# One half of a convolution moved from matmul taps to passes on VectorE, and a row of scales turned one step later

## The chip, the cores and the metric

The kernel runs on one core of a Trainium2 chip. The metric is the time of one execution on the device in microseconds (us). Every comparison takes executions of both kernels on the same chip in the same rounds. The runs of the kernel before lay 0.2 to 0.4% apart within one call (3428.75 to 3435.80 us in the closest, 3426.04 to 3440.02 us in the widest); the record lists every run used here as fast.

Engine names are the profile's: PE is TensorE (matmul), DVE is VectorE, ACT is ScalarE, POOL is GpSimd, SP is SyncE, which issues the transfers here. "px", "pb", "ls_in" and the like are tiles of the program. Line numbers (L938) are lines of the kernel in question and shift by a few between kernels.

## The reference, cut to what matters

The kernel computes two layers on a 4 x 128 x 64 x 64 input. The change lies in the middle: a two-directional state-space block on 4 sequences of 4096 tokens with 128 channels. For each direction:

```python
def _mamba3(x, in_proj, conv_w, conv_b, A_log, dt_bias, D, norm_w, out_proj):
    zxbcdt = x @ in_proj                                # 128 -> 256 (z) + 256 (x) + 64 (B) + 64 (C) + 4 (dt)
    z, xbc, dt = jnp.split(zxbcdt, [D_INNER, D_INNER + CONV_DIM], axis=-1)
    xp = jnp.pad(xbc, ((0, 0), (K - 1, 0), (0, 0)))
    conv = sum((xp[:, i:i + l, :] * conv_w[:, i] for i in range(K))) + conv_b      # K = 4 taps
    xbc = jax.nn.silu(conv)
    xh, Bm, Cm = jnp.split(xbc, [D_INNER, D_INNER + D_STATE], axis=-1)
    ...                                                 # dt, decays, the scan over chunks, gate, norm
t = t + (mamba(ln(t), fwd) + reversed(mamba(reversed(ln(t)), bwd)))
```

The 256 channels of x are two halves of 128, in two directions: four "halves of x" to be projected and convolved. A depthwise convolution behind a projection can be made in two ways. PE can run one matmul per tap, with the tap multiplied into the weights, on shifted inputs (four matmuls, no other work). Or PE projects once, and DVE adds the shifted, scaled copies (one matmul, one eviction on ACT, three passes on DVE).

## The kernel before: the parts that matter

The block runs as 128 steps of 128 tokens (32 steps, i = 0 to 31, for each of 4 sequences). Four steps j = 0 to 3 are a group; while a group is scanned, the projections of the next one are made. All projections and several small tiles share three PSUM buffers in turn (`ring`). The orders of PE and ACT are the program's; the orders of DVE and POOL are chosen by a scheduler when the kernel is built, and then fixed.

```python
def row_scales(nc, k, ps, tag, pool, src, mr, mem, parts=None):
    yield from row_statistics(nc, k, ps, tag, pool, src, mr, parts)   # ls_in: four transposes, then bn_stats on DVE
    n = mr.shape[1]
    pt = ps.tile([n, P], F32, tag=tag, name="rs_t")                   # the turn of the scales
    nc.tensor.transpose(pt, mr[:, :, 1], k.ident)
    ...                                                               # copied, written to DRAM

def open_sequence(b):                     # a generator: one piece per step, from i = 4 of the sequence before
    ...
        yield from row_scales(nc, k, ring, "big", wk, src, mr, mem)   # i = 4..7 statistics, i = 8 turn
        scales(b, mem)                                                # 8 transfers tl <- scale
        for _ in range(3):
            yield
    if b not in ready:
        yield from scaled(b)                                          # 8 products tl x t on POOL
        yield
    yield from steps(b, ready[b])                                     # the "dt work": pd, pdt, pcs, pr

# forward halves: four tap matmuls each
def project_fwd(gr, c):
    px = ring.tile([P, MG], F32, tag="big", name="px")
    for tap in range(KC):
        nc.tensor.matmul(px, w[0]["x"][:, tap, bass.ts(c, P)], tl[:, rows(g, 0, tap)], ...)
    nc.scalar.activation(gr["x"][0][:, c, :], px, AF.Silu, bias=...)

# backward halves: one matmul, three passes
def project_bwd(gr, c):
    px = ring.tile([P, MG], F32, tag="big", name="px")
    nc.tensor.matmul(px, w[1]["x"][:, bass.ts(c, P)], tl[:, rows(g, 1, PAD)], start=True, stop=True)
    ...                                                               # memset, eviction, 3-column addition
    for n in range(1, KC):
        v = x[:, PAD - n : PAD - n + MG]
        nc.vector.scalar_tensor_tensor(v, px, taps[:, PAD - n : KC - n], v, ALU.mult, ALU.add)

# the deal over the steps of a group
if j == 0:   project_bwd(next, 0); project_bc(next, 0); project_fwd(next, 0)
elif j == 1: project_bwd(next, 1); means(...); project_bc(next, 1)
elif j == 2: project_fwd(next, 1); activate_bwd(next); project_z(...) x 4
```

In every step PE runs the state matmul, four transposes of x, the product y from lt and xdt, the product y from ct and S, and then "small" (L991), which must wait until DVE has updated the state S (L1029). Three sequences out of four are prepared during the one before (row statistics, turn, scaling, dt work: i = 4 to 21), and after a sequence has ended its output's row statistics are taken for the last layer (i = 20 to 28 of the next one, `ended`).

## Time and profile before

| | before |
|---|---|
| time, median of the rounds with the changed kernel | 3436.31 us (3430.04 to 3440.71, 4 runs) |
| span of the profiled run, granted clock | 3440.8 us, 0.980 |
| recurrent part | about 1934 to 3275 us |
| PE / DVE busy over the span | 95% / 62% |

The busy shares only say that PE is nearly always at work. What PE waits for is in the view of waits. Here it is for the recurrent part, 1935 to 3225 us of the kernel before (waiting line, what released it, us in total, times, longest):

```profile
PE small L991 <- DVE S L1029: 15.1, 29, 1.4
PE pdt L821 <- DVE xT L938: 8.1, 3, 2.7
PE ls_in L83 <- DVE xT L938: 7.0, 5, 2.0
...
PE pr L879 <- DVE ms L1089: 5.4, 3, 2.6
```

All the waits listed in this view total 55 us of 1290. What costs is which of them are long: pdt and pr are dt work, three times each (once for each coming sequence), and the clock falls behind them: after the wait of 2.71 us for pdt at 2123.76 us four transposes took 1.11 us, after one of 1.04 us at 2332.39 us they took 0.66 us (both in the profile lines of the prediction, below). "Half speed" and "half clock" stand below for such stretches, in which PE's instructions took 1.7 to 1.8 times as long as at other times (the y product from lt in the same step 1.98 us, otherwise 1.09); "full speed" stands for the other times.

A group's length is taken here from the start of its first px to the start of the next group's. Undisturbed groups of the last sequence take 39.7 to 40.3 us; those with row statistics 43 to 46; those in which dt work runs 49 to 51.

### The profile page before, as it was taken

Reading aid. Unit: us, or ns where it says so; the run is one execution under the profiler, and the core shown is the slowest. Engines: PE = TensorE matmul, PEld = TensorE weight load, DVE = VectorE, ACT = ScalarE, POOL = GpSimd, SP = SyncE. Lnnn points to the kernel's source line nnn. Section 1 sums busy time; section 2 is a strip of 40 time slices with the busy share of each in tenths; the row PEclk is TensorE's granted clock in tenths of the full one; section 3 lists DMA queues with packets and bytes.
Section 4 is the critical chain, followed back from the end, with each engine's and each line's share of the span. In section 5 each row is a group of like instructions: output and inputs, shape, how many; then the busy total and the mean of one; then the engine's idle time right before and its main releaser. Section 6 shows DMA issues by size and latency. Waiting matters only on the chain. (4 is left out here: it accounts for less than half of the span.)

```text
span 3440.8 us, 43618 instructions
## 1 busy us (share of the span) xinstructions
PE 3261.0 (95%) x16823; PEld 1717.0 (50%) x16823; DVE 2138.7 (62%) x3204; ACT 1557.9 (45%) x2060; POOL 1593.3 (46%) x1414
## 2 busy tenths in 40 slices
PE   7999999999999999999998899999999999999976
PEld 2554545555555555455554344444444444544445
DVE  7555445555545555455544676777677777777767
ACT  3323233323333333333322566666656566666556
POOL 3434332534343424242533265557446654565653
PEclk9999999999999999999999899999999999999988
DMA  4000000000000000000001233333333423333332
GB/s 164 1 1 1 1 1 1 0 1 1 1 1 1 0 1 1 1 1 1 1 1 48 74 111 80 96 87 111 86 81 96 111 80 81 95 94 89 85 109 99
DMA packets 91685, 162.71 MB, mean 47 GB/s; under 512 B 23822, under 2 KB 27534, under 8 KB 90316
## 3 DMA queue, kind: packets, MB, share of 16 engines
q1 hardware_dynamic: 90252, 158.53, 16.2%
q8 instruction: 134, 2.20, 0.3%
q10 hardware_dynamic: 1216, 1.31, 0.1%
q14 instruction: 83, 0.68, 0.1%
HBM read 149.97 MB, written 9.82 MB: 46 GB/s over the span
## 5 line engine op out<-in xcount | busy, mean ns | idle before, releaser
L369 ACT ACTIVATE ex<-pf 128x1024 f32<-128x1024 f32 x512 | 497.0, 1021 | 571.6 <-PE pf L367 559.3
L384 DVE TENSOR_TENSOR es<-es,ex 128x1024 f32<-128x1024 f32 x448 | 590.6, 1318 | 207.5 <-ACT ex L369 179.4
L367 PE MATMUL pf<-theta,phi 64*128 64x512 f32 x2048 | 513.3, 619 | 10.8 <-ACT ex L369 10.4
L319 PE MATMUL pm<-yf,w 128*128 128x256 f32 x2048 | 503.1, 380 | 0.0
L378 PE MATMUL acc<-ex,gT 128*64 128x512 f32 x2048 | 491.4, 606 | 0.2 <-ACT ex L369 0.2
L331 POOL TENSOR_TENSOR eo<-s 128x256 f32<-128x256 f32 x128 | 90.1, 725 | 782.4 <-ACT s L328 782.4
L319 PEld LDWEIGHTS pm<-yf,w 128*128 128x128 f32 x2048 | 383.9, 189 | 113.5 <-issue 54.3
L367 PEld LDWEIGHTS pf<-theta,phi 64*128 64x128 f32 x2048 | 174.0, 186 | 326.7 <-ACT ex L369 208.6
L1007 POOL TENSOR_TENSOR ct<-ct,Cst 128x512 f32<-128x512 f32 x128 | 181.3, 1417 | 323.0 <-DMA ct<-csmem 261.9
L334 DVE TENSOR_TENSOR eo<-eo,pm 128x512 f32<-128x512 f32 x64 | 44.0, 688 | 425.8 <-PE pm L319 397.1
L378 PEld LDWEIGHTS acc<-ex,gT 128*64 128x64 f32 x2048 | 127.5, 136 | 337.5 <-issue 327.2
L969 DVE TENSOR_TENSOR lt<-cs,lt 128x1024 f32<-128x1024 f32 x128 | 180.5, 1411 | 182.3 <-DMA lt<-csmem 171.7
L328 ACT COPY s<-pm 128x512 f32<-128x512 f32 x64 | 37.5, 585 | 498.6 <-PE pm L319 498.6
L286 POOL TENSOR_TENSOR yf<-yr 128x340 f32<-128x340 f32 x256 | 241.4, 963 | 4.9
L914 PE MATMUL px<-tl,wx_fwd 128*128 128x512 f32 x512 | 238.6, 609 | 0.0
L901 PE MATMUL pb<-tl,wbc_bwd 128*64 128x512 f32 x512 | 235.1, 601 | 0.0
L901 PE MATMUL pb<-tl,wbc_fwd 128*64 128x512 f32 x512 | 234.5, 601 | 0.0
L286 POOL TENSOR_TENSOR yr<-xp 128x700 f32<-128x700 f32 x64 | 100.4, 1569 | 277.8 <-PE pm L319 232.0
L1072 POOL TENSOR_TENSOR yT<-yT,zT 128x512 f32<-128x512 f32 x127 | 183.8, 1456 | 74.1 <-DVE yT L1059 58.7
L1006 DVE TENSOR_TENSOR lt<-lt,gm 128x1024 f32<-128x1024 f32 x128 | 187.6, 1465 | 1.3
L390 DVE RECIPROCAL att<-den 128x512 f32<-128x512 f32 x32 | 107.4, 3357 | 108.0 <-PE den L388 108.0
L319 PE MATMUL pm<-yr,w 128*128 128x256 f32 x512 | 162.6, 398 | 0.0
(263 smaller groups left out, 5488.1 us busy)
## 6 DMA issues: line engine op xcount, KB each, us to landing
lt<-csmem SPq DMA_DIRECT2D x128, 512.0 KB, 5.5
ct<-csmem SPq DMA_DIRECT2D x256, 128.0 KB, 5.3
rs<-m SPq DMA_DIRECT2D x31, 512.0 KB, 3.7
t<-in_x SPq DMA_DIRECT2D x4, 2048.0 KB, 28.5
rows<-after SPq DMA_DIRECT2D x32, 256.0 KB, 4.8
out<-t SPq DMA_DIRECT2D x4, 2048.0 KB, 11.4
tl<-scale SPq DMA_DIRECT2D x24, 256.0 KB, 6.4
w<-in_w7t SPq DMA_DIRECT2D x1, 3136.0 KB
```

The source lines that it names most:

```text
L286: nc.gpsimd.tensor_tensor(out, at(x), at(y), op)
L319: nc.tensor.matmul(pm[:, e, :], wt, src, start=(i == 0), stop=(i == len(terms) - 1))
L367: nc.tensor.matmul(pf[:, e, :], phi[HALF[e], m, :], th[HALF[e]], start=True, stop=True)
L369: nc.scalar.activation(ex, pf, AF.Exp, scale=scale)
L378: nc.tensor.matmul(acc[HALF[e]], gT[:, 2 * m + e, :], ex[:, e, :], start=(m == 0), stop=(m == NT // 2 - 1))
L384: nc.vector.tensor_tensor(es, es, ex, ALU.add)
L901: nc.tensor.matmul(out, w[i]["bc"][:, tap, bass.ts(c, DS)], src, start=(tap == 0), stop=(tap == KC - 1),)
L914: nc.tensor.matmul(px, w[0]["x"][:, tap, bass.ts(c, P)], tl[:, rows(g, 0, tap)], start=(tap == 0), stop=(tap == KC - 1),)
L969: nc.vector.tensor_tensor(m["lt"], m["b"]["cs"][:, :, m["i"], :].unsqueeze(3).to_broadcast([P, ND, NHEAD, P]), m["lt"], ALU.subtract,)
L1006: nc.vector.tensor_tensor(lt, lt, gm.unsqueeze(2).to_broadcast([P, ND, NHEAD, P]), ALU.mult)
L1007: nc.gpsimd.tensor_tensor(m["ct"], m["ct"], Cs[:, cols].unsqueeze(1).to_broadcast([P, NHEAD, P]), ALU.mult)
L1072: eng.tensor_tensor(v, v, gr["z"][d][:, :, half(d, j // 2)], ALU.mult)
```

## The change

The intent was to take 192 matmul instructions off PE, which is busy 95% of the span, give DVE the three passes instead, and to let the scales' turn come a step later, when its input is sure to be there. The diff, cut to its core:

```diff
 def row_scales(...):
     yield from row_statistics(nc, k, ps, tag, pool, src, mr, parts)
+    yield
     n = mr.shape[1]
...
-        def project_fwd(gr, c):
+        def project_fwd(gr):                      # forward half 0 alone keeps four taps
...
-        def project_bwd(gr, c):
+        def project(gr, i, c):                    # backward 0 and 1, forward 1
+            wx = w[1]["x"][:, bass.ts(c, P)] if i else w[0]["x1"]
+            nc.tensor.matmul(px, wx, tl[:, rows(g, i, PAD)], start=True, stop=True)
...
             for n in range(1, KC):
-                nc.vector.scalar_tensor_tensor(v, px, taps[:, PAD - n : KC - n], v, ALU.mult, ALU.add)
+                nc.vector.scalar_tensor_tensor(at(n), px, taps[:, PAD - n : KC - n], at(n), ALU.mult, ALU.add)
...
             if j == 0:
-                    project_bwd(groups[G + 1], 0)
+                    project(groups[G + 1], 1, 0)
+                    project(groups[G + 1], 0, 1)
                     project_bc(groups[G + 1], 0)
-                    project_fwd(groups[G + 1], 0)
...
             elif j == 2:
-                    project_fwd(groups[G + 1], 1)
-                    activate_bwd(groups[G + 1])
+                    project_fwd(groups[G + 1])
+                    for i, c in STEPS_X:          # (1, 0), (0, 1), (1, 1)
+                        activate(groups[G + 1], i, c)
```

The one added `yield` sits in a generator. Everything after it in the same generator moves one step later too: the eight transfers of the scales, the eight products on POOL, and the dt work. So the change has two parts: the convolution (C), and the delay (Y), which is itself three delays for each coming sequence. The same helper also turns the scales for the last layer (`ended`); those turns move one step as well, and so do the scales of the first sequence, before the loop.

More of the change, by code (lines that the diff above doesn't have):

```diff
@@ L762, in mamba @@
                 s["z"] = wp.tile([P, DI], F32, name="wz_" + d)
-                s["x"] = wp.tile([P, DI] if i else [P, KC, DI], F32, name="wx_" + d)
+                s["x"] = wp.tile([P, DI] if i else [P, KC, P], F32, name="wx_" + d)
                 s["bc"] = wp.tile([P, KC, 2 * DS], F32, name="wbc_" + d)
@@ L770, in mamba @@
                     if i == 0:
-                        nc.gpsimd.tensor_tensor(s["x"][:, c, :], f[:, DI : 2 * DI], cw[i][:, c, 0:DI], ALU.mult)
+                        nc.gpsimd.tensor_tensor(s["x"][:, c, :], f[:, DI : DI + P], cw[i][:, c, 0:P], ALU.mult)
                 if i:
                     nc.scalar.copy(s["x"], f[:, DI : 2 * DI])
+                else:
+                    s["x1"] = wp.tile([P, P], F32, name="wx1")
+                    nc.scalar.copy(s["x1"], f[:, DI + P : 2 * DI])
                 nc.scalar.copy(s["z"], f[:, 0:DI])
@@ L906, in project_bc @@
             act() if later is None else later.append(act)
-        def project_fwd(gr, c):
+        def project_fwd(gr):
             tl, g = gr["tl"], gr["at"][1]
-            if c == 0:
-                gr["x"][0] = grp.tile([P, 2, MG], F32, tag="x0", name="xT0")
             px = ring.tile([P, MG], F32, tag="big", name="px")
             for tap in range(KC):
-                nc.tensor.matmul(
-                    px, w[0]["x"][:, tap, bass.ts(c, P)], tl[:, rows(g, 0, tap)],
-                    start=(tap == 0), stop=(tap == KC - 1),
-                )
-            nc.scalar.activation(gr["x"][0][:, c, :], px, AF.Silu, bias=w[0]["cb"][:, c : c + 1])
@@ L920, in project_bwd @@
-        def project_bwd(gr, c):
+                nc.tensor.matmul(px, w[0]["x"][:, tap, :], tl[:, rows(g, 0, tap)], start=(tap == 0), stop=(tap == KC - 1))
+            nc.scalar.activation(gr["x"][0][:, 0, :], px, AF.Silu, bias=w[0]["cb"][:, 0:1])
+        def project(gr, i, c):
             tl, g = gr["tl"], gr["at"][1]
-            if c == 0:
-                gr["x+"] = grp.tile([P, 2, PAD + MG], F32, tag="x1", name="xT1")
-                gr["x"][1] = gr["x+"][:, :, PAD:]
             px = ring.tile([P, MG], F32, tag="big", name="px")
-            nc.tensor.matmul(px, w[1]["x"][:, bass.ts(c, P)], tl[:, rows(g, 1, PAD)], start=True, stop=True)
-            x = gr["x+"][:, c, :]
-            taps = w[1]["taps"][:, c, :]
-            nc.vector.memset(x[:, 0:PAD], 0.0)
-            nc.scalar.activation(x[:, PAD:], px, AF.Identity, scale=taps[:, PAD:KC], bias=w[1]["cb"][:, c : c + 1])
+            wx = w[1]["x"][:, bass.ts(c, P)] if i else w[0]["x1"]
+            nc.tensor.matmul(px, wx, tl[:, rows(g, i, PAD)], start=True, stop=True)
+            x = gr["x+"][i][:, c, :]
+            taps = w[i]["taps"][:, c, :]
+            at = lambda n: x[:, PAD - n : PAD - n + MG] if i else x[:, n : n + MG]
+            nc.vector.memset(x[:, 0:PAD] if i else x[:, MG:], 0.0)
+            nc.scalar.activation(at(0), px, AF.Identity, scale=taps[:, PAD:KC], bias=w[i]["cb"][:, c : c + 1])
@@ L933, in project_bwd @@
             if g:
-                v = x[:, MG : MG + PAD]
-                nc.vector.tensor_tensor(v, v, groups[gr["at"][0] * NG + g - 1]["x+"][:, c, 0:PAD], ALU.add)
+                v = x[:, MG:] if i else x[:, 0:PAD]
+                past = groups[gr["at"][0] * NG + g - 1]["x+"][i][:, c, :]
+                nc.vector.tensor_tensor(v, v, past[:, 0:PAD] if i else past[:, MG:], ALU.add)
             for n in range(1, KC):
-                v = x[:, PAD - n : PAD - n + MG]
-                nc.vector.scalar_tensor_tensor(v, px, taps[:, PAD - n : KC - n], v, ALU.mult, ALU.add)
@@ L940, in activate_bwd, with activate @@
-        def activate_bwd(gr):
-            for c in range(2):
-                x = gr["x"][1][:, c, :]
-                nc.scalar.activation(x, x, AF.Silu)
+                nc.vector.scalar_tensor_tensor(at(n), px, taps[:, PAD - n : KC - n], at(n), ALU.mult, ALU.add)
+        def activate(gr, i, c):
+            x = gr["x"][i][:, c, :]
+            nc.scalar.activation(x, x, AF.Silu)
         def project_z(gr, i, c):
@@ L1102, in means @@
             )
+        STEPS_X = ((1, 0), (0, 1), (1, 1))
         def outputs(gr, d):
@@ L1174, in open_group @@
         def open_group(G):
-            groups[G] = dict(at=(G // NG, G % NG), tl=ready[G // NG], x={}, bc={}, z={}, y=([], []))
+            x = [grp.tile([P, 2, PAD + MG], F32, tag=f"x{i}", name=f"xT{i}") for i in range(ND)]
+            groups[G] = {
+                "at": (G // NG, G % NG), "tl": ready[G // NG], "bc": {}, "z": {}, "y": ([], []), "x+": x,
+                "x": [x[0][:, :, 0:MG], x[1][:, :, PAD:]],
+            }
         def open_step(n):
@@ L1194, in mamba @@
             act()
-        for c in range(2):
-            project_bwd(groups[0], c)
-        for c in range(2):
-            project_fwd(groups[0], c)
-        activate_bwd(groups[0])
+        for i, c in STEPS_X:
+            project(groups[0], i, c)
+        project_fwd(groups[0])
+        for i, c in STEPS_X:
+            activate(groups[0], i, c)
         differences(m[0])
@@ L1235, in mamba @@
                 if more:
-                    project_bwd(groups[G + 1], 1)
+                    project(groups[G + 1], 1, 1)
                 if G > 0:
@@ L1242, in mamba @@
                 if more:
-                    project_fwd(groups[G + 1], 1)
-                    activate_bwd(groups[G + 1])
+                    project_fwd(groups[G + 1])
+                    for i, c in STEPS_X:
+                        activate(groups[G + 1], i, c)
                 for i in range(ND):
```

## The prediction

> **What bounds the kernel now.** I read the page first, then the busy time stretch by stretch, then the groups of instructions, and last the timelines of TensorE (PE) and VectorE (DVE) in one group of the part that the change touches, with the chain that ended last beside them.
>
> ```profile
> PE 3261.0 (95%) x16823; PEld 1717.0 (50%) x16823; DVE 2138.7 (62%) x3204; ACT 1557.9 (45%) x2060; POOL 1593.3 (46%) x1414
> 2000.00:2400.00 400.00, 383.52 (x2526) 196.16 (x2526) 296.73 (x544) 248.77 (x331) 239.69 (x186) 0.99 0.36 99
> ```
>
> The first line is the whole span. The second is one stretch of the recurrent part (about 1935 to 3300 us, the only part the change touches apart from the moved turn of the scales); its columns are length, then busy PE, PE weight load, DVE, ACT, POOL, then granted clock, DMA share and GB/s. There PE is busy 383.5 of 400 us and DVE already 296.7 (74%). So PE bounds the part, but DVE has only a quarter free, and the average hides single steps. The part is 32 groups of four steps. In each group the convolved x of the next group is made: the forward half by four tap matmuls each, the backward halves by one matmul and three passes on DVE.
>
> ```profile
> L914 PE MATMUL px<-tl,wx_fwd 128*128 128x512 f32 x509 | 237.3, 609 | 0.0
> L938 DVE SCALAR_TENSOR_TENSOR xT<-px,taps_bwd,xT 128x512 f32<-128x512 f32 x192 | 142.7, 745 | 7.2 <-ACT xT L932 4.2
> ```
>
> A logical tap matmul shows as two instructions (32 groups x 2 halves x 4 taps x 2 = 512). Next, the chain through a group's first step (start, us, what), and DVE in the same step:
>
> ```profile
> 2231.71 0.26 PE small L991
> 2231.97 0.42 PE small L993 x4
> 2232.39 1.06 PE px L928 x2
> 2233.45 3.60 PE pb L901 x16
> 2237.04 3.63 PE px L914 x8
> ...
> 2243.46 0.26 PE small L991
> ```
>
> ```profile
> 2231.81 2.06 DVE L969 TENSOR_TENSOR lt<-cs,lt 128x1024 f32<-128x1024 f32 x1
> 2236.76 1.63 DVE L969 TENSOR_TENSOR lt<-cs,lt 128x1024 f32<-128x1024 f32 x1
> 2238.31 0.74 DVE L938 SCALAR_TENSOR_TENSOR xT<-px,taps_bwd,xT 128x512 f32<-128x512 f32 x1
> 2241.37 0.42 DVE L1029 TENSOR_TENSOR S<-S,small 128x256 f32<-128x256 f32 x1 [2.32 <-PE small L1017]
> ```
>
> PE takes 11.75 us from one L991 to the next with no gap. The next L991 needs the state update S (L1029) on DVE; S waited 2.32 us for PE and ended at 2241.79, 1.67 us before PE wanted it. DVE's slack in this step is therefore 2.32 + 1.67 = 4.0 us. In the second and third step there is none: PE is tied to the transfer of lt (the chain has a DMA of 5.3 to 5.7 us there, followed by DVE work and then PE).
>
> [...]
>
> ```profile
> 2123.76 1.11 PE L821 MATMUL pdt<-ident,pds 128*128 128x128 f32 x4 [2.71 <-DVE xT L938]
> 2124.81 1.12 PE L1017 MATMUL small<-xdtd,bt 128*64 128x256 f32 x4
> ...
> 2332.39 0.66 PE L83 MATMUL ls_in<-ident,t 128*128 128x128 f32 x4 [1.04 <-DVE xT L938]
> 2332.98 0.65 PE L1017 MATMUL small<-xdtd,bt 128*64 128x256 f32 x4
> ...
> 3261.86 0.40 PE L101 MATMUL rs_t<-ident,mr 128*32 128x128 f32 x1 [5.38 <-POOL mr L74]
> ```
>
> After 1.04 us idle four transposes take 0.66 us; after 2.71 us they take 1.11 and everything is slow for some 5 us, which adds 2.5 to 3 us. [...] beside GpSimd's additions L969 took 2.06 and 1.63 us instead of 1.23, while the passes with px in PSUM (L938) stay at 730 to 755 ns throughout. [...] the passes here follow each other at 0.66 us (2238.31 to its end is 0.74, the next row could start earlier), so I use 0.66 us on the path.
>
> **The change part by part.** Forward half 1 loses three of four taps: 3 x 2 instructions at 0.43 us (eight L914 in 3.63 us less the fill, L901 pairs start every 0.43) = 2.58 us of PE per group, 82.6 us over 32. That is the ceiling, 2.4%. Against it, per group: DVE gains three passes (3 x 0.745), a three-column addition (0.16 alone) and a memset (0.06) = 2.5 us; ACT gains 0.78 (Identity eviction) + 0.62 (Silu in place) − 0.69 (Silu eviction) = 0.71 us. DVE then holds about 30 + 2.5 = 32.5 us of a group of some 37.4, so what counts is which step gets it.
>
> First step. PE work is now one px, one px, pb: 11.75 − 2.58 = about 9.1 us. By the built program's order, DVE runs between two S: xdt, xdtd, lt difference, gm, the lt product, a pass, a second lt difference, then four passes (two per projection, taken in turns), then S; the sixth pass follows S. The second difference cannot start before its transfer, 5.1 us after the first L991 (2236.76 − 2231.64), takes 1.6, then 4 x 0.66 and S 0.4: 9.8 us. So the step becomes DVE-bound at about 9.85 us: gain 1.9, not 2.58.
>
> Second step: the same PE work, with the sixth pass at its start, where DVE has waited 3.2 us for a transfer. All passes but one now come after S, and the next px (third step) takes the PSUM buffer that they read: it can start 0.1 us sooner to 0.3 later. About 0.
>
> Third step: px for forward half 0 and the four z. The fourth z waits for the eviction of the first, behind three instead of two in-place Silu: +0.57 us on ACT, of which about 0.4 reach PE. Loss 0.4. Fourth step unchanged.
>
> A group without row statistics: 1.9 − 0.4 = 1.5 to 1.6 us. There are 22 such among the 31 that project for a successor: 22 x 1.6 = +35 us.
>
> Nine groups also take row statistics (three with two sets a step, six with one). There PE transposes four blocks (ls_in) after the projections, in one of three PSUM buffers. Before, that buffer was released early in the first step, because 3.6 us of forward taps lay between. Now PE arrives 6.2 us after L991 and the buffer is the first projection's, read until its third pass, about 8.8 to 9.2 us. PE idles some 2.9 us, past the length that cost the clock above; then four transposes, state, turn and y run at half speed. First steps of 12.2 to 12.6 us become about 15. Nine times −2.7 = −24 us.
>
> Before the loop: weights on GpSimd halved (3.72 us for four, PE waited 1.89 for them) and six matmuls less at a cold clock, nine passes instead of six: about +3 us.
>
> The moved turn of the scales: only at 3261.86 did it cost anything, 5.38 us idle and about 3 us of slow clock; one step later the input is ready: +8 us. It also moves the dt work of a sequence one step later, off the step where it waited 2.7 us for passes, onto ones where it waits for others: 0.
>
> Sum: 35 − 24 + 3 + 8 = 22 us. 3434.6 − 22 = about 3412 us, −0.65%.
>
> **The rivals.** (a) All of PE's saving counts: 82.6 + 8 = 91 us, 3344 us. For it: PE is busy 96%, and the 4.0 us of DVE slack exceeds the 2.5 added. Against: PE's own shortening of 2.58 uses up that slack too (4.0 − 2.58 − 1.7 before S is below zero). (b) DVE becomes the bound everywhere: each group loses what the first step gains and statistics groups lose 3 to 4 us with the clock: 3450 to 3460. For it: 74% average, several DVE instructions stretched to 2.3 us by GpSimd. Against: in plain groups DVE still waits 2 to 3 us for transfers in three of four steps. (c) The clock stays up[...]: statistics groups lose 0.5 instead of 2.7, 3392.
>
> **Range and chances.** The sum rests on 35 ± 12 and −24 ± 14[...]. I take 3412, with 3382 to 3440 for 8 in 10. Faster by over 2% (below 3365.9) needs nearly all of the ceiling: 0.05. Slower by over 2% (above 3503) would need DVE to bind in every step and the clock to fall in most: 0.02. Within: 0.93.
>
> **What would show it right or wrong.** Right: PE matmul instructions fewer by 192; plain groups of about 38 us instead of 39.7; in their first step L991 waits for S (L1028 in the changed kernel) by up to 1 us; in statistics groups ls_in waits 2.5 to 3.5 us for a pass on px, and the four transposes after it take 1.1 us; no wait of 5 us before the last turn of the scales. Wrong: plain groups at 37.2 us (then DVE had more room than I counted), or over 39 us (then the third step's px waits for the passes), or statistics groups at the old 43 to 46 us.

## The result, and the profile after

| | before | after |
|---|---|---|
| median (range, runs) | 3436.31 us (3430.04 to 3440.71, 4) | 3410.97 us (3404.29 to 3415.20, 4) |
| profiled span, clock | 3440.8 us, 0.980 | 3412.4 us, 0.977 |

The ratio of after to before is 0.9926, 95% interval 0.9901 to 0.9951. Ratios here are the mean time of one kernel's fast runs over that of the other's in the same rounds, so not quite the ratio of the medians. The time, 25 us less, is almost exactly the predicted 3412; it falls in the class "within 2%", which was given 0.93. The terms of the sum are another matter.

The page of after, busy time of the span:

```profile
PE 3188.1 (93%) x16631; PEld 1685.0 (49%) x16631; DVE 2194.7 (64%) x3360; ACT 1573.9 (46%) x2090; POOL 1610.2 (47%) x1414
```

The stretch 2000 to 2400 us of after (length, PE, weight load, DVE, ACT, POOL, granted clock, DMA share, GB/s):

```profile
2000.00:2400.00 400.00, 365.50 (x2467) 187.69 (x2467) 312.45 (x589) 251.09 (x336) 245.73 (x189) 0.97 0.37 99
```

PE has exactly 192 instructions fewer (16823 to 16631). It is busy 18 us less in this stretch and DVE 16 us more, and the granted clock has gone from 0.99 to 0.97. PE now waits longer (98 us in all the waits listed for 1935 to 3225 us, 55 in before), and after some of its waits it runs at half speed, as the lines further down show.

The group of instructions that was moved, in after: DVE's passes by tile (busy, mean ns, idle before).

```profile
L938 DVE SCALAR_TENSOR_TENSOR xT<-px,taps_bwd,xT 128x512 f32<-128x512 f32 x192 | 141.7, 738 | 4.3 <-ACT xT L932 4.0
L938 DVE SCALAR_TENSOR_TENSOR xT<-px,taps_fwd,xT 128x512 f32<-128x512 f32 x96 | 70.8, 738 | 0.0
```

The 96 new passes take 70.8 us of DVE, each 738 ns, like the old ones. Four in a row start 0.66 us apart (3034.34, 3035.00, 3035.66 and 3036.32 us in the step below).

An undisturbed plain group's first step in after (steps 8 to 11 of the last sequence; start, duration, instruction, idle time before it), first PE, then DVE in the same step:

```profile
3028.05 1.13 PE L927 MATMUL px<-tl,wx_bwd 128*128 128x512 f32 x2
3029.02 1.02 PE L927 MATMUL px<-tl,wx 128*128 128x512 f32 x2
...
3033.45 0.61 PE L1016 MATMUL small<-xdtd,bt 128*64 128x256 f32 x4
...
3037.44 0.33 PE L990 MATMUL small<-ident,Bst 128*128 128x128 f32 x1 [1.17 <-DVE S L1028]
```

```profile
3034.34 0.74 DVE L938 SCALAR_TENSOR_TENSOR xT<-px,taps_bwd,xT 128x512 f32<-128x512 f32 x1
...
3036.32 0.74 DVE L938 SCALAR_TENSOR_TENSOR xT<-px,taps_fwd,xT 128x512 f32<-128x512 f32 x1
3036.97 0.41 DVE L1028 TENSOR_TENSOR S<-S,small 128x256 f32<-128x256 f32 x1
3037.30 0.74 DVE L938 SCALAR_TENSOR_TENSOR xT<-px,taps_fwd,xT 128x512 f32<-128x512 f32 x1
```

The state matmul that S needs ends at about 3034.06. S starts only at 3036.97, right behind four passes, and PE waits 1.17 us for it. The step shrank from 11.76 us to 10.07, and the group from 39.72 to 38.64.

The waits of PE in after, same window as before:

```profile
PE ls_in L83 <- DVE xT L938: 27.4, 11, 3.4
PE small L990 <- DVE S L1028: 23.8, 18, 2.8
PE y L1046 <- POOL ct L1006: 18.4, 3, 6.3
```

The first two were expected. The third was not: three waits of 6 us for a product on POOL, one in each sequence during which the next one is prepared. What stands ahead of that product on POOL, and the issue of the transfers on SP:

```profile
2034.73 7.23 SPq L110 DMA_DIRECT2D tl<-scale  x8
2042.36 1.09 SPq L961 DMA_DIRECT2D ct<-csmem  x2
```

```profile
2042.36 5.25 POOL L728 TENSOR_TENSOR tl<-tl,t 128x512 f32<-128x512 f32 x4 [8.97 <-DMA tl<-scale]
...
2052.13 2.12 POOL L728 TENSOR_TENSOR tl<-tl,t 128x512 f32<-128x512 f32 x2
...
2054.79 1.26 POOL L1006 TENSOR_TENSOR ct<-ct,Cst 128x512 f32<-128x512 f32 x1
```

All eight products of the delayed scaling run from 2042.36 to 2054.2, and the ct product that PE needs comes behind them, at 2054.79. PE gets it at 2056.1, after 6.31 us idle, and then runs at half speed for about 5 us (this y product took 1.13 us, otherwise 0.67; the two px matmuls at 2058.30 took 2.07 us, otherwise 1.13). The transfer of ct is not what it waited for: its second half was issued at 2042.99, and the page of after has a median of 5.3 us from issue to landing of ct, so it was there at about 2048.3 (an estimate from these two numbers). What stood in the way is POOL's order: an idle wait of 8.97 us for the transfers of the scales, and then the products.

Two more lines of after, for the row statistics in a first step and for the last turn (PE):

```profile
1975.06 1.09 PE L83 MATMUL ls_in<-ident,t 128*128 128x128 f32 x8 [3.14 <-DVE xT L938]
1976.08 1.12 PE L1016 MATMUL small<-xdtd,bt 128*64 128x256 f32 x4
...
3234.29 1.11 PE L83 MATMUL ls_in<-ident,t 128*128 128x128 f32 x4 [4.24 <-POOL t L1150]
...
3242.29 0.30 PE L102 MATMUL rs_t<-ident,mr 128*32 128x128 f32 x1
```

The wait of 3.14 us and the half clock behind it (1.12 us where 0.65 is full speed) are as predicted. The last turn (rs_t) no longer waits 5.38 us, but the row statistics of the last sequence in the step where it used to stand now wait 4.24 us for an addition on POOL, and PE runs at half speed behind it (1.11 us for the four transposes, otherwise 0.66).

The table that carried the rest of the study adds up group lengths of the profiled runs by place in the sequence, over the sequences listed (the last group listed is that of steps 20 to 23 of the last sequence). "Start" is the start of the first group; it moved by up to 5 us between runs with the same convolution code before it, so that much of a profile's span is scatter. Each column is one execution, and not always a typical one: the profiled execution took 6.3 us more than the median of its kernel in before (3442.57 us), 3.3 more in after, 10.4 more in "+ late turn", 4.1 less in "dt later", and lay within 2 us of it in the other four. A few us in one row are therefore no evidence by themselves.

| steps | before | after | Y alone | C alone | dt later | C + dt later | + late turn | S first, plain |
|---|---|---|---|---|---|---|---|---|
| 0-3 | 156.0 | 157.2 | 155.6 | 156.7 | 155.5 | 159.0 | 157.7 | 156.8 |
| 4-7 | 176.7 | 178.8 | 177.2 | 181.4 | 177.6 | 177.4 | 180.5 | 177.0 |
| 8-11 | 163.5 | 173.9 | 171.1 | 158.6 | 162.5 | 160.4 | 173.9 | 157.9 |
| 12-15 | 161.8 | 165.2 | 167.2 | 159.1 | 159.5 | 159.1 | 164.0 | 157.9 |
| 16-19 | 191.5 | 165.5 | 175.1 | 194.7 | 179.1 | 162.9 | 162.5 | 159.6 |
| 20-23 | 185.2 | 183.9 | 187.3 | 169.0 | 186.0 | 183.9 | 187.4 | 185.8 |
| 24-27 (3 sequences) | 126.7 | 123.6 | 126.8 | 124.4 | 126.9 | 124.4 | 122.7 | 121.8 |
| 28-31 (3 sequences) | 117.3 | 111.6 | 117.3 | 109.6 | 116.0 | 110.2 | 111.8 | 110.1 |
| sum | 1278.9 | 1259.6 | 1277.6 | 1253.4 | 1263.1 | 1237.3 | 1260.6 | 1226.8 |
| start | 1934.1 | 1927.8 | 1929.6 | 1929.8 | 1929.3 | 1930.7 | 1932.8 | 1930.1 |

Before to after, the largest entries are not where the convolution should act: 26 us gained in steps 16 to 19, 14 us lost in steps 8 to 15. That gave theory R: Y is two opposite effects, the dt work moved to better steps and the scaling moved ahead of a ct product. Its rival is P, the sum as predicted: Y worth 8 us at the last turn, nothing else.

### The profile page after: what moved, and what is told of

It is laid out like the page before. It is cut to its first block, busy times and chain, and to the rows that moved or that the text cites. A ratio compares the mean times of both kernels' runs of the same rounds, so it can differ in the third digit from the quotient of the medians.

```text
span 3412.4 us, 43419 instructions
## 1 busy us (share of the span) xinstructions
PE 3188.1 (93%) x16631; PEld 1685.0 (49%) x16631; DVE 2194.7 (64%) x3360; ACT 1573.9 (46%) x2090; POOL 1610.2 (47%) x1414
## 5 line engine op out<-in xcount | busy, mean ns | idle before, releaser
L368 PE MATMUL pf<-theta,phi 64*128 64x512 f32 x2048 | 511.9, 618 | 12.4 <-ACT ex L370 12.0
L1006 POOL TENSOR_TENSOR ct<-ct,Cst 128x512 f32<-128x512 f32 x128 | 207.5, 1621 | 318.2 <-DMA ct<-csmem 281.3
L329 ACT COPY s<-pm 128x512 f32<-128x512 f32 x64 | 37.5, 585 | 496.9 <-PE pm L320 496.9
L968 DVE TENSOR_TENSOR lt<-cs,lt 128x1024 f32<-128x1024 f32 x128 | 172.8, 1350 | 124.8 <-DMA lt<-csmem 124.6
L1071 POOL TENSOR_TENSOR yT<-yT,zT 128x512 f32<-128x512 f32 x127 | 175.2, 1388 | 60.5 <-DVE yT L1058 44.8
L1038 PE MATMUL y<-lt,xdt 128*64 128x128 f32 x2048 | 146.4, 287 | 6.6 <-DVE lt L1005 3.4
```

What stands on the lines that cost most here:

```text
L368: nc.tensor.matmul(pf[:, e, :], phi[HALF[e], m, :], th[HALF[e]], start=True, stop=True)
L968: nc.vector.tensor_tensor(m["lt"], m["b"]["cs"][:, :, m["i"], :].unsqueeze(3).to_broadcast([P, ND, NHEAD, P]), m["lt"], ALU.subtract,)
L1006: nc.gpsimd.tensor_tensor(m["ct"], m["ct"], Cs[:, cols].unsqueeze(1).to_broadcast([P, NHEAD, P]), ALU.mult)
L1038: nc.tensor.matmul(y[HALF[h], d, c, at[d]], m["dt"][:, d, 2 * c + h, :], m["lt"][:, d, 2 * c + h, :], start=(i % 2 == 0 and c == 0), stop= ...
L1071: eng.tensor_tensor(v, v, gr["z"][d][:, :, half(d, j // 2)], ALU.mult)
```

## The experiments

Twelve kernels ran in four calls, each call on one chip with its own runs of the kernel before. Later calls are compared with "C + dt later" through the ratios to before.

### 1. Y alone

```diff
 # kernel before
     yield from row_statistics(nc, k, ps, tag, pool, src, mr, parts)
+    yield
```

> The kernel before with nothing but the one-step delay of the scales (no work of x moved). Theory P, the sum in the prediction: the delay is worth about 8 us (a wait of 5.4 us at the last turn and about 3 us of slow clock behind it), and neither the dt work nor the multiplication by the scales matters, so about 3428 us, ratio 0.9977. Theory R, read from the trace of after: the delay moves three things of one chain, and gains about 25 us in the groups of steps 16 to 19 (dt work), loses about 16 us in the groups of steps 8 to 15 (C waits about 6 us for GpSimd behind the scaling), and gains about 8 us at the end: about 3417 to 3421 us, ratio 0.995 to 0.9965. R also expects two or three waits of some 6 us of the y product for the C product on GpSimd; P expects none.

Measured: 3435.18 us against 3434.09 of before; ratio 1.0009 (0.9996 to 1.0023). The delay is worth nothing, so both theories were too hopeful. The column shows why it is zero: 16.4 us gained in steps 16 to 19, 13.0 lost in steps 8 to 15, 2.1 lost in steps 20 to 23. The loss that R named is there, but not by the wait that it named: there is no wait for ct in this run's view of waits. Another instruction stands behind the delayed scaling here, the first half of S's update (L1027). POOL, then DVE, in steps 8 to 11 of the first sequence of this kernel:

```profile
2049.85 3.18 POOL L728 TENSOR_TENSOR tl<-tl,t 128x512 f32<-128x512 f32 x3
2052.99 0.61 POOL L1027 TENSOR_TENSOR S<-S,tot 128x256 f32<-128x256 f32 x1
```

```profile
2053.64 0.42 DVE L1030 TENSOR_TENSOR S<-S,small 128x256 f32<-128x256 f32 x1 [3.57 <-POOL S L1027]
```

DVE waited 3.57 us for POOL's half of S, and PE then 3.44 us for S. In both kernels something that PE needs stands behind the delayed scaling on POOL; which instruction it is, the scheduler decides.

### 2. C alone

```diff
 # kernel after
     yield from row_statistics(nc, k, ps, tag, pool, src, mr, parts)
-    yield
```

> The kernel after without the delay of the scales: only the convolution of forward half 1 moved to VectorE and the new deal. Theory P (sum of the prediction: +35 in 22 groups, -24 in nine, +3 at the start): gain 14 us, about 3422 us, ratio 0.996. Theory R (23 plain groups of about 1.2 to 1.5 us gained where nothing else runs, groups with row statistics about 0 to 2 us lost, 6 us at the start): gain 5 to 15 us, 3421 to 3431 us, with the groups of steps 16 to 19 still at about 50 us in the sequences with dt work, and no wait for the C product on GpSimd in the groups of steps 8 to 11.

Measured: 3412.30 us; ratio 0.9943 (0.9929 to 0.9956), 22 us less. So the convolution alone has nearly the whole gain of the change (after: 25 us in its own rounds), more than the 14 that P gave it (the interval of the ratio is 15 to 24 us) and more than R's 5 to 15. Steps 16 to 19 stay at 50 us and more in three sequences, as R expected, and no wait for ct is in its view of waits. The 16 us gained in steps 20 to 23 were expected by neither.

Against before, two waits are gone from these groups: that of pr in the second step (2.61 us in the second sequence), and that of the row statistics behind it (2.00 us, after which the four transposes took 1.11 us). No wait of pr is listed in this run; why it went was not tested. Against after, a piece of dt work (pcs, pt) stands in the first step, and gives PE something to do, and the ring two more buffers, between the projections and the row statistics. PE in the group of steps 20 to 23 of the second sequence, this run:

```profile
2491.75 0.66 PE L83 MATMUL ls_in<-ident,t 128*128 128x128 f32 x4 [0.22 <-DVE xT L937]
...
2503.11 0.66 PE L83 MATMUL ls_in<-ident,t 128*128 128x128 f32 x4 [0.41 <-ACT Cst L909]
```

The two sets of transposes waited 2.10 and 1.92 us in after, and the same group took 48.7 us there and 42.7 here. In experiment 4, which differs from this run in the place of the dt work alone, they waited 2.10 and 1.91 us and the group took 49.0. But in the first step of steps 16 to 19 C alone pays for it: pd, the first piece of dt work, takes the buffer of the first px and waits for its passes, which it did not do before:

```profile
PE pd L815 <- DVE xT L937: 8.5, 3, 3.0
```

### 3. Only the dt work later

```diff
 # kernel before, in open_sequence
         yield from scaled(b)
         yield
+        yield
     yield from steps(b, ready[b])
```

> The kernel before with only the dt work of the next sequence one step later; the turn of the scales and the multiplication by them stay where they were. Theory P gives this part nothing: 3436 us. Theory R puts the whole gain of the groups of steps 16 to 19 (about 25 us) on it and none of the loss in the groups of steps 8 to 15: about 3410 to 3414 us, ratio 0.993, which is as fast as the whole change. If it gains less than 10 us, the gain at steps 16 to 19 comes from something else (the last piece of scaling moved, or the new deal).

Measured: 3427.20 us; ratio 0.9984 (0.9970 to 0.9997), 7 us less. The gain in steps 16 to 19 is there (12.4 us) with no loss in steps 8 to 15, so its cause is the place of the dt work; but it is half of what R said, and below the "10 us" that R had set itself in the times. The waits did not get smaller: pd waits at the new place as long as pdt did at the old one (8.1 us in three times in before).

```profile
PE pd L811 <- DVE xT L938: 7.9, 3, 2.7
```

Part of the gain may be the clock behind these waits. In the second and third sequence pd waited nearly the same, 2.66 and 2.62 us; after the first PE ran at half speed (four transposes in 1.1 us), after the second at full speed, and the groups took 48.0 and 44.9 us.

### 4. C and only the dt work later

```diff
 # C alone, in open_sequence
         yield from scaled(b)
         yield
+        yield
```

> The convolution part of the change, with the dt work one step later, but the turn and the scaling left where they were. Theory P: 3422 us (convolution alone, dt work worth nothing). Theory R: the sum of convolution alone and dt work later, about 30 to 40 us, so 3396 to 3406 us and faster than the kernel after by 5 to 15 us, with no wait of about 6 us for the C product on GpSimd.

Measured: 3396.02 us (3389.75 to 3403.84); ratio 0.9891 (0.9877 to 0.9905), 38 us less than before and clearly below the changed kernel's ratio of 0.9926. The parts are not additive. With the convolution as it was, moving the dt work is worth 7 us; with C it is worth 16 (3412.30 to 3396.02). The table shows where: with C, steps 16 to 19 gain 31.8 us and steps 20 to 23 lose 14.9; without C they gain 12.4 and lose 0.8. C made the old place only 3.2 us worse (194.7 against 191.5); the larger part is that the new place is cheaper with C (162.9 against 179.1), and there no wait of pd is listed any more. Why the passes come in time there was not tested. This kernel is the base of what follows. Two of its waits are needed below:

```profile
PE ls_in L83 <- DVE xT L937: 28.1, 11, 3.5
PE small L989 <- DVE S L1027: 22.8, 18, 2.3
```

### 5. The late turn put back

```diff
 # C + dt later, in open_sequence
-                yield from row_scales(nc, k, ring, "big", wk, src, mr, mem)
+                yield from row_scales(nc, k, ring, "big", wk, src, mr, mem, late=True)   # one yield before rs_t
                 scales(b, mem)
-                for _ in range(3):
+                for _ in range(2):
                     yield
```

> The fastest so far (convolution moved, dt work one step later, scales turned at the old step: 3396 us) plus only the turn of a coming sequence's scales one step later, with everything behind it (the dt work) left where it is in that kernel, and the turn for the last layer left at the old step. Theory R: the late turn alone causes the loss of the groups of steps 8 to 15, because its transfers and the eight multiplications on GpSimd then stand ahead of one C product: y waits about 6 us for that C product three times, the groups of steps 8 to 11 grow from about 40.5 to about 45 us and those of 12 to 15 by about 2, in three sequences: +13 to +20 us, so 3409 to 3416 us. Rival: the loss comes from the change in convolution or from the position of the dt work: within 3 us of 3396, no wait of 6 us.

Measured: 3412.53 us; ratio 0.9938 (0.9925 to 0.9951), against 0.9891: 16 us lost. Most of it is in steps 8 to 15 (18.4 of the 23.3 us by which the column's sum exceeds that of the base), and the wait is back, in the view of waits of this kernel:

```profile
PE y L1047 <- POOL ct L1007: 18.7, 3, 6.3
```

R is shown here: the late turn of the coming sequence's scales alone costs 16 us. (The column exceeds the base by more than that, as its profiled execution was the slowest of the five, 3422.95 us.) The eight products keep their written step in this run; what is later is their input, and the scheduler still sets all eight ahead of the ct product. Because dt work later gains 16 with C and the late turn loses 16, Y is worth next to nothing in the changed kernel: 25 us with it and 22 without (experiment 2), in intervals that overlap.

### 6. Only the last turn late

```diff
 # C + dt later
 def ended(b):
-    return row_scales(..., mr, after[b])
+    return row_scales(..., mr, after[b], late=True)
```

> The fastest so far (3396 us) plus only the turn of the scales for the last layer one step later (in the three sequences that have one). Theory P (the prediction's term): the wait of 5.9 us before the last turn and about 3 us of slow clock behind it go: -8 us, 3388 us. Theory R: the row statistics of the same step stand right behind that turn and wait for an addition to t on GpSimd, so 3.5 to 4.3 us of the wait stay there and the clock still drops: -1 to -3 us, 3393 to 3395 us.

Measured: 3395.16 us; ratio 0.9886 (0.9870 to 0.9902) against 0.9891, no difference that these rounds can show. The trace of "C + dt later" has a wait of 5.87 us before the last rs_t; this one has none there and 4.22 us before the row statistics, for t on POOL (first line: "C + dt later", second: this run).

```profile
3216.76 0.40 PE L101 MATMUL rs_t<-ident,mr 128*32 128x128 f32 x1 [5.87 <-POOL mr L74]
3218.40 1.11 PE L83 MATMUL ls_in<-ident,t 128*128 128x128 f32 x4 [4.22 <-POOL t L1151]
```

As R said, the wait went to the next instruction in the step that needs POOL.

### 7. The added passes taken away (wrong result on purpose)

```diff
 # C + dt later, in project
-            for n in range(1, KC):
+            for n in range(1, KC if i else 1):     # no passes for forward half 1
```

> WRONG RESULT ON PURPOSE: the fastest so far (3396 us) without the three passes on VectorE for forward half 1 (everything else stays: one projection, memset, eviction, Silu). It measures what the added passes cost. Theory P (VectorE binds the first step, and the passes hold the buffer that the row statistics need): plain groups fall from 38.5 to about 37.3 us (23 x 1.2 = 28 us) and the nine groups with row statistics by 1 to 4 us each (waits of 2 to 3.4 us at the row statistics fall below 1.5): 40 to 55 us less, 3341 to 3356 us. Rival: the passes are nearly free and PE or the transfer of lt sets the 38.5 us: less than 15 us gained, above 3381 us.

Measured: 3383.54 us; ratio 0.9857 (0.9842 to 0.9871), some 12 us less than with the passes. The result is wrong, as intended. In the last sequence, plain groups take 37.5 us instead of 38.5, close to the 37.3 that P said of them. The groups with row statistics did not follow: the eight listed got shorter by only 1.9 us together, where P expected 1 to 4 us of each. Two groups of steps 4 to 7 even grew by 3 and 5 us. So the added passes cost 1.0 us in a plain group, and next to nothing certain elsewhere. In total the rival was right (above 3381 us), but not with its reason, that the passes are nearly free everywhere.

### 8. The B projection first where row statistics follow

```diff
 # C + dt later, first step
+                    early = b > 0 and g in (5, 6)
+                    if early:
+                        project_bc(groups[G + 1], 0)
                     project(groups[G + 1], 1, 0)
                     project(groups[G + 1], 0, 1)
-                    project_bc(groups[G + 1], 0)
+                    if not early:
+                        project_bc(groups[G + 1], 0)
```

> The fastest so far (3396 us), but in the six groups where one block of row statistics for the last layer runs in the first step, the B projection stands before the two projections of x, so the row statistics take the buffer of B (free after one eviction) and not that of x (held until its third pass). Theory P (term of 2.7 us per group: a wait of about 2.9 us plus the clock): the waits of 2.1 to 3.45 us of these transposes for a pass go, and 2 to 3 us of each group with them: -12 to -18 us, 3378 to 3384 us. Theory R2: the wait only moves to the next instruction on PE that needs VectorE (small for S, because the passes start later by 3 us and the statistics now stand among them): within 5 us of 3396.

Measured: 3416.62 us; ratio 0.9956 (0.9940 to 0.9973) against 0.9891: 22 us slower, worse than either theory. Waits of this kernel:

```profile
PE small L989 <- DVE S L1027: 51.8, 23, 8.2
PE ls_in L83 <- DVE xT L937: 13.3, 5, 3.9
```

The waits of the row statistics fell from 28.1 us in 11 times to 13.3 in 5, as P wanted. The waits for S rose from 22.8 to 51.8. With the statistics' input there early, the scheduler set their work and all six passes before S on DVE: in the last sequence S started 6.5 us after its matmul had ended, and PE waited 4.70 us. One reading is that in the base the wait on ls_in hid work that DVE had to do before S in any case; taking it away moved it to S. The edit also puts the two projections, and so the start of the passes, behind the B projection, 3.6 us of PE; how much of the loss is due to that was not separated.

### 9. S before the last passes

The passes are written into the program after the next step's update of S, or at the moment when another tile wants their buffer.

```diff
 # C + dt later, in project
-            for n in range(1, KC):
-                nc.vector.scalar_tensor_tensor(at(n), px, ...)
+            ring.put_off(passes)                   # 3-column addition and the three passes
 # in the loop
             S1 = states(m[n], S)
+            ring.flush()
```

> The fastest so far (3396 us), with the passes written into the program after the next step's update of S, or at the moment when their buffer is wanted by another matmul. In the built program VectorE's order in a plain group's first step changes from four passes before S to two before and two after; the groups with row statistics keep theirs, since there the buffer is wanted earlier. Theory R (what is left of the plain groups' possible gain, 38.5 instead of 37.3 us, is S queued behind passes that nobody waits for yet): L989 no longer waits 1 to 1.2 us for S, plain groups fall to about 37.6 us: 13 to 16 groups x 0.9 = -10 to -16 us, 3380 to 3386 us. Rival (VectorE's total work sets the step, so the wait comes back at the passes' readers in the second step: px for its buffer, or y for lt): within 4 us of 3396.

Measured: 3402.97 us; ratio 0.9918 (0.9905 to 0.9932), about 9 us slower than the base, which neither theory had. The mechanism worked: plain groups of the last sequence fell from 38.5 to 37.5 us. The gain was eaten elsewhere; in the waits of this kernel a line stands that was 2.3 us in 3 times in the base:

```profile
PE rs_t L101 <- DVE xT L959: 11.4, 5, 2.7
```

The turns of scales follow the projections in the first step, take the buffer of the first px and so wait for passes that had been put off. The two groups of steps 28 to 31 affected grew by 4.6 and 2.9 us. The profiled execution was the fastest of the five (3396.80 us), and its groups sum to 1235.8 us against 1237.3 in the base; so the trace shows why nothing was gained, but not where the other executions lost 9 us.

### 10. The dt work two steps later, on top of 9

```diff
 # run 9, in open_sequence
         yield from scaled(b)
         yield
         yield
+        yield
```

> The run with S first, with the dt work of the coming sequence one step later again (two steps later than in the kernel before), so that its transposes stand in the third and fourth step of a group, where no passes run. Theory R (what the dt work costs is set by which step it lands in: beside passes it finds its PSUM buffer held and the clock drops): the groups of steps 20 to 23 in two sequences fall from about 49 to about 44 us, the groups of steps 16 to 19 stay at about 41: -8 to -12 us against the run with S first. Theory P (the prediction: moving the dt work is worth nothing): no change beyond 2 us.

Measured: 3398.39 us; ratio 0.9898 (0.9883 to 0.9913) against 0.9918; the intervals overlap. Steps 20 to 23 fell by 4.3 us in sum, less than the 8 to 12 that R named. Inconclusive.

### 11. S first, in plain groups only

```diff
 # run 9
+            ring.now = (b + 1 < B and g in (1, 2)) or (b > 0 and g >= 5)   # there: passes at once, as in the base
```

> S first as in the run before, but only in groups where no row statistics and no turn of scales follow the projections; in the others the passes are written as in the fastest so far (3396 us). Theory R (S first gains 1.0 us in each plain group; what ate it in the run before were turns of scales and row statistics that found their PSUM buffer held longer by the passes put off): the groups of steps 28 to 31 return from 41.5 and 39.7 to about 36.9 us, the plain groups of the last sequence stay at 37.5: -10 to -13 us against the fastest so far, 3383 to 3387 us. Rival (the gain is within what the slow clock takes elsewhere from run to run, some 5 us, or VectorE's total work binds): 3392 to 3400 us.

Measured: 3385.61 us (3380.14 to 3386.28); ratio 0.9851 (0.9834 to 0.9867), against 0.9891 of the base and 0.9926 of the changed kernel. It lies in the range that R gave (3383 to 3387). This is the fastest correct kernel: 49 us below before in its own rounds. An undisturbed group's first step, DVE and then PE:

```profile
3007.74 0.73 DVE L961 SCALAR_TENSOR_TENSOR xT<-px,taps_fwd,xT 128x512 f32<-128x512 f32 x1
3008.39 0.41 DVE L1053 TENSOR_TENSOR S<-S,small 128x256 f32<-128x256 f32 x1
3008.72 0.74 DVE L961 SCALAR_TENSOR_TENSOR xT<-px,taps_bwd,xT 128x512 f32<-128x512 f32 x1
```

```profile
3006.34 0.61 PE L1041 MATMUL small<-xdtd,bt 128*64 128x256 f32 x4
...
3009.08 0.33 PE L1015 MATMUL small<-ident,Bst 128*128 128x128 f32 x1
```

S now has two passes directly before it instead of four, and the second "small" follows without a wait. The first step takes 8.84 us (3000.93 to 3009.77 from px to px), and the group 37.5 us, the same as in experiment 7 without the added passes. So in a plain group the passes cost nothing once S does not stand behind them.

### 12. Run 11 with the dt work two steps later

```diff
 # run 11, in open_sequence
         yield from scaled(b)
         yield
         yield
+        yield
```

> The run above with the dt work one step later once more. The trace of the earlier run with both showed the groups of steps 20 to 23 shorter by 4.3 us in sum over three sequences and those of steps 8 to 11 longer by 2 (where nothing was moved, so scatter). Theory R: -3 to -8 us against the run above. Theory P (the dt work's step is worth nothing): within 2 us.

Measured: 3386.23 us (3383.11 to 3397.79); ratio 0.9865 (0.9842 to 0.9887) against 0.9851. No gain. One step later takes the dt work off its bad place; a second step adds nothing that these rounds show.

## Why the prediction was right, and by which steps it was not

The total was right to 1 us, and the direction of the main term, the convolution, was right. Of the four terms of "35 - 24 + 3 + 8 = 22", none could be confirmed at its size; that their sum came out is luck.

**"Moved turn of the scales: +8", "dt work: 0".** This is the step that failed in its reasoning, although the two together came out near: predicted 8, measured 0 (experiments 1 and 2). The dt work's place is worth 16 us with the convolution moved and 7 without. The prediction saw the 2.7 us waits of pdt and assumed other waits of the same size at the new place. Without C that was so (7.9 us in three against 8.1), and yet the groups got shorter; with C no wait of pd was left there. The late turn of a coming sequence's scales costs 16 us, through POOL's order and the transfers it waits for, which the prediction did not look at: it left the scaling out of its sum and never asked what stands behind it in POOL's fixed order. In the trace of after the ct product at 2054.79 us ran only behind eight products that began at 2042.36 us. SP took 7.23 us there for the eight issues of the scales' transfers, 0.90 us each, where the median from issue to landing is 7.0 us, and the ct transfers next in SP's order were issued only behind all eight; in before the same eight took 4.01 us. And the gain of 8 us at the last turn was not there: the wait of 5.4 to 5.9 us became one of 4.2 us at the next instruction that needed POOL (experiment 6).

**"A group without row statistics: 22 x 1.6 = +35".** The mechanism was right, and the size was off. In the undisturbed group shown, the first step gained 1.69 us (predicted 1.9), the second lost 0.10 (predicted 0), the third lost 0.51 (predicted 0.4), the fourth nothing: 1.08 in all. With C alone the 22 groups gained 16.4 us, in after 17.2, and there the sum mixes the convolution with what Y moves (against C alone, after gains 29.2 us in steps 16 to 19 and loses 21.4 in steps 8 to 15). What kept the first step at 10.07 us was called DVE-bound; experiment 11 shows that it was not DVE's amount of work but the place of S behind four passes.

**"Nine statistics groups: -24".** Of the nine, eight are listed; they gained 9.1 us with C alone and 2.1 in after. The waits came as said: 11 times, 1.9 to 3.4 us. Two things were left out. The clock fell less often than assumed: of the 11 waits between 1.9 and 3.43 us in after, four (1.91, 2.34, 2.39 and 3.43 us) were followed by full speed right through the next y product (1.09 us in each of the four). And the groups already paid for such waits before: in steps 4 to 7 of the first sequence the first step lost 2.1 us, but the second gained 0.9, because a wait of 1.04 us for a pass there had gone, and the fourth 0.4. The loss was counted in one step and the group's other steps were taken as unchanged. So the sign that the prediction had set itself came out mixed: in after, steps 4 to 7 took 46.4 to 47.1 us (45.0 to 45.9 in before), but the two listed groups of steps 24 to 27 with statistics took 41.6 (43.3 and 43.7 in before). With C alone, dt work between the projections and the row statistics hid two of the waits altogether (experiment 2).

**"Before the loop: +3".** The profile shows 6.3 us, but Y alone and dt later alone, which do not touch that part, began 4.6 and 4.8 us earlier too. It can't be read from these runs. The slow clock that it counts there is in the trace of before: the two px matmuls at 1912.28 us took 2.08 us (1.13 in the loop), and the 16 forward taps after them 9.11 us (3.70 for eight in the loop).

One reading of the prediction goes beyond its source, though no term rests on it. The chain of before has 22 transfers of lt, at most one in a group, and all but two start in a group's first step; in the group that the prediction quotes there is none, and its second and third step (2243.46 to 2263.60) are PE work but for 0.3 us.

Set against the measurements, the sum is then: convolution 22 us by experiment 2 (predicted 35 - 24 + 3 = 14) and Y 0 (predicted 8). The error of one term was the other's, with the opposite sign: that is the luck. Rival (a), all of PE's saving (82.6 us by the prediction's working), falls: even without the passes the kernel stayed at 3384. Rival (b), 3450 to 3460, falls with the measured 3411; the stretched DVE instructions that it names are there (in the recurrent part of before L969 took 1.21 to 1.23 us in the 20 cases with POOL idle beside it, and up to 2.34 us with POOL busy), but not in the passes (L938, 0.73 to 0.755 us throughout). Rival (c), a clock that stays up, explains part of the difference in the statistics groups: after four of the 11 waits PE ran at full speed.

What stays open: how much of the difference in steps 20 to 23 (48 to 49 us in "C + dt later", 42.7 in C alone, in two sequences) is the waits and how much the half clock behind them, which none of these runs separates (the one pair that can be compared, in experiment 3, differs by 3.1 us); and when exactly the clock falls. In before, all five steps that held waits of 1.9 to 2.72 us (seven waits, two steps with two each) ran at half speed after them; in after, four of the 11 row-statistics waits of 1.9 to 3.43 us were not followed by it. Single waits of 1.92 and 2.10 us in after were, and one of 3.43 us was not: the length of a single wait does not tell.

## What to carry to other kernels

When one delay moves a generator or a queue, list every piece that moves with it and look at what each engine, also one that is mostly idle, and the transfer queue have behind that piece in their fixed order; test the pieces apart, because gains and losses of the same size can cancel (16.4 us against 13.0 and 2.1 in experiment 1). Work added to an engine with slack costs little if the one instruction that another engine waits for does not stand behind it: check its place in the built order before counting busy time (a plain group took 37.5 us with the passes in experiment 11 and 37.5 without them in experiment 7, but 38.5 with S behind four of them). A wait that is taken away at one instruction can come back at the next that needs the same engine (5.87 us became 4.22 in experiment 6), and can be larger there (in experiment 8 the row statistics' waits fell by 14.8 us, those for S rose by 29.0).
